# A written-out start, fillers on TensorE, and a chunk scan in steps of 4, 4, 4 and 2: one block of adaLN, state space and experts

## The chip, the core and the metric

The kernel runs on one core of a Trainium2 chip. The metric is device time in microseconds (us); lower is better. All data is float32.

## What is computed

Eight sequences of 512 tokens with 256 features each pass through two parts. Each part is wrapped in a modulation: six vectors per sequence are made of a conditioning row c, and the input is normalised, scaled, shifted, and the result is gated and added back.

```
mod = (silu(c) @ wmod).reshape(8, 6, 1, 256)          # sa ca ga sb cb gb
ga, gb = sign(ga) * max(|ga|, 0.25), the same for gb
h = layernorm(x) * (1 + ca) + sa
x = x + ga * mamba(h)
h = layernorm(x) * (1 + cb) + sb
x = x + gb * experts(h)

mamba(x):  xn = layernorm(x) * gamma + beta
           u, z = split(xn @ W_in.T)                    # 512 and 512
           xc = silu(causal_conv(u, 4 taps) + conv_b)
           state = state @ A.T + u_t @ Bm.T             # 16 numbers, 512 steps
           y_t = (xc_t + state @ Cm) * sigmoid(z_t)
           return x + y @ W_out.T
experts(x): softmax router over 8, the best one's two-layer gelu network, times a gate
```

## The kernel before

**Two halves.** The first half works on one sequence at a time ("batch" b, 0 to 7): `stage_norm` (L735, normalise, modulate, normalise, transpose to `xnT`), `stage_base` (L759, the residual and the gated output weights), `stage_conv` (L774, the state scan and the convolution), `stage_out` (L824, gate, output projection `po`, router) and `stage_place` (L899, where each token goes for its expert). The second half works through blocks of 256 or 128 tokens that belong to one expert: gather rows, two layers (`ph`, `py`), scatter the result. TensorE (PE) does the matmuls, VectorE (DVE) and ScalarE (ACT) the elementwise work and the emptying of PSUM, GpSimd (POOL) powers, residuals and the indirect DMAs, SyncE (SP) issues all other DMAs.

**The scan.** The 512 steps are cut into 128 chunks of CH = 4. `pv` gives each chunk's own contribution, 32 rows by 128 chunks, four of them stacked in `v`. What enters each chunk is then summed in steps with `SPAN` = (8, 4, 4) (L428, loop at L792): in the first step `pd` adds up the 8 chunks before each one with eight matmuls (weights `wb`), in the second three gaps of 8, 16, 24 chunks, in the third three gaps of 32, 64, 96 (weights `lm`). Each step ends with a DVE addition of `pd` into `v`, which the next step's matmuls read. `pc` then turns `v` into outputs. For weights the kernel needs powers of A: `states()` (L590) squares A repeatedly (`pa` into `at`), forms a few products more (`pmo`, `pm28`, into `more`), and lays them out (`lt`, `wb`, `lx`, `lm`, `cs`, `bw`). `pq`, `pw1`, `pm2`, `pw` and `pb` are the PSUM tiles of these.

**The modulation.** `three()` (L482) multiplies by one half of `wmod` (tiles `wm`): `pm` holds shift and scale, `pg` the gate. It is called for batch 0 alone on all partitions (`bc0`, from `s0`), and in `vectors()` (L513) for all eight rows, once per half; these go to memory as `mod_d` and `modb_d`. `stage_norm(b)` fetches its row of `mod_d` into `bc`. `vectors()` also computes sb, cb and ga with the features on the partitions (`pf`, six pieces of 128 features, two accumulating matmuls each, into `modT`), from which router weights `rw`, `rsum` and, by way of `wo` transposed, `pr` and `wr2`, come.

**Rows for the experts.** `xp_d` holds, per token, the row `xr` made by `stage_out` and a copy of the sequence's three modulation vectors, which a DMA from `modb_d` writes for a whole sequence at once (1536 KB). Before the change batch 0 issues those of sequences 0 and 1, batch b that of b + 1. The gathers of the first expert blocks, after batch 5, read what belongs to sequences 0 to 5.

**What sets the order.** Nothing is in the order of the code. The class `Plan` (L32) records every instruction of a half with a due time, what it depends on, and an estimated length (L92). `order()` (L191) then runs through them like a simulation: among the instructions whose inputs are there and whose buffer is free, the one that could start earliest is taken, and with equal starts the one due first. Each engine then executes its instructions in just that order. `nc.wanting(done=[...])` makes the planner wait for a tile as if the instruction read it. Batch b is due at (b + 3) * 36 us; `states()` and `vectors()` stand first, with a due time of 1e6 that what follows brings forward. PSUM tiles are taken by tag: `px` has three buffers, `tp` and `po` two each, `ps` one.

Of the kernel before, what the change touches and what calls it, by code (L numbers as in the profile page):

```python
# [35 lines left out]
class Plan:  # L36
# [20 lines left out]
    def __init__(self, tc, last=None):  # L57

        self.tc, self.nc = tc, tc.nc
        self.free = {q: last.free[q] if last else 0.0 for q in self.REACH}  # L60
        self.ops, self.touched, self.tiles = [], {}, {}
        self.due, self.also, self.pairing = 0.0, ([], []), 0
        for name in self.QUEUES:
            setattr(self, name, self.Engine(self, name))
# [71 lines left out]
    def add(self, name, op, args, kw):  # L136
# [19 lines left out]
        else:  # L156
# [6 lines left out]
            self.ops.append(me)  # L163
        if op == "activation":
            me["table"] = {AF.Gelu: 1, AF.Silu: 2, AF.Tanh: 2}.get(args[2] if len(args) > 2 else None)
        if "dma" in op:
            me["size"] = 4
            for _, n in out.ap:
                me["size"] *= n
            me["indirect"] = "indirect" in op  # L170
# [20 lines left out]
    def order(self):  # L191
# [19 lines left out]
        order, table = [], 2  # L211
# [14 lines left out]
        while len(order) < len(ops):  # L226
            best = None
            for q, l in ready.items():
                for o in l:
# [6 lines left out]
                    if best is None or (at, o["due"]) < best[:2]:  # L236
                        best = (at, o["due"], o)
            assert best is not None, "no buffer for any instruction that could be next"
            at, _, o = best
            table = o.get("table") or table  # L240

# [6 lines left out]
            free[o["queue"]] = at + o["length"]  # L248
            end = at + o["length"]
# [40 lines left out]
def adaln_mamba_moe_kernel(  # L290
# [137 lines left out]
    SPAN = (8, 4, 4)  # L428
    assert SPAN[0] * SPAN[1] * SPAN[2] == NC

    with tc.tile_pool(name="wa", bufs=1) as wa, tc.tile_pool(
# [81 lines left out]
        def vectors():  # L513

            for half, to in ((0, mod_d), (1, modb_d)):
                mod = wa.tile([B, 3, D], FP, name=f"mod{half}", tag="mod")
                three(mod, sT, half, B)
                nc.sync.dma_start(out=to, in_=mod.rearrange("b i d -> b (i d)"))


            pf = ps_o.tile([P, 6, B], FP, name="pf", tag="po")
            for m in range(6):
                w, at_m = (wmh[1], m) if m < 4 else (wmh[0], m)
                for k in range(KD):
                    nc.tensor.matmul(
                        pf[:, m], lhsT=w[:, k, at_m * P : (at_m + 1) * P],
                        rhs=sT[:, k, :], start=(k == 0), stop=(k == KD - 1),
                    )
            nc.vector.tensor_copy(modT[:, 0:2], pf[:, 0:2])
            nc.vector.tensor_scalar(modT[:, 2:4], pf[:, 2:4], 1.0, None, ALU.add)  # L530
            gT = modT[:, 4:6]
            nc.vector.tensor_copy(gT, pf[:, 4:6])
            mT = wa.tile([P, KD, B], FP, name="mT")
            nc.vector.scalar_tensor_tensor(mT, gT, -1.0, gT, ALU.mult, ALU.max)
            nc.vector.tensor_scalar(mT, mT, 0.25, None, ALU.max)
            nc.vector.tensor_scalar(gT, gT, 0.0, 2.0, ALU.is_ge, ALU.mult)
            nc.vector.scalar_tensor_tensor(gT, gT, -1.0, mT, ALU.add, ALU.mult)
# [52 lines left out]
        def states():  # L590


            for j in range(STEPS - 1):
# [5 lines left out]
                nc.vector.tensor_copy(at[:, j + 1], pa)  # L599
# [4 lines left out]
            nc.vector.tensor_copy(a3t, pa3)  # L604
# [6 lines left out]
            for i in range(CH):  # L611
                for j in range(i + 1):
                    nc.vector.tensor_copy(lt[:, i, j * SP : j * SP + DS], power[i - j])
                nc.vector.tensor_copy(lt[:, i, DS : 2 * DS], power[i + 1])
# [6 lines left out]
            more = wa.tile([DS, 6, DS], FP, name="more")  # L621
            pmo = ps_s.tile([DS, 5, DS], FP, name="pmo", tag="ps")
            for i, (l, r) in enumerate((
                (at[:, 3, 0], at[:, 2, 1]), (at[:, 4, 0], at[:, 2, 1]), (at[:, 4, 0], at[:, 3, 1]),
                (at[:, 6, 1], at[:, 5, 0]), (at[:, 8, 1], at[:, 7, 0]),
            )):
                nc.tensor.matmul(pmo[:, i], lhsT=l, rhs=r, start=True, stop=True)
            nc.vector.tensor_copy(more[:, 0:5], pmo)
            pm28 = ps_s.tile([DS, DS], FP, name="pm28", tag="ps")
# [759 lines left out]
```

## Time and profile before

| | us |
|---|---|
| median of 3 runs | 589.22 |
| lowest, highest | 585.32, 590.69 |
| the profiled execution | 587.33 |
| its span, first to last instruction | 585.2 |
| PE busy in the span | 562.3 |
| last `po` matmuls of batch 0 begin | 79.06 |
| last `po` matmuls of batch 7 begin | 313.46 |

The profile is of one execution. Its page has the span in 40 equal slices of 14.6 us, a digit giving tenths; "PEclk" is the TensorE clock that was granted. Timelines give start and duration in us, the engine, the line of the code that issued the instruction, the tiles and their shapes. All instructions that a plan records carry the line of the helper that records them (L154 or L159), so they are told apart by their tiles.

### The profile page before, as it was taken

What the parts mean: (1) busy time and instruction counts of PE and PEld (TensorE: products, weight loads), DVE (VectorE), ACT (ScalarE), POOL (GpSimd) and SP (SyncE); (2) the same over time, 40 slices, a digit from 0 to 9 for tenths busy, and PEclk for the clock granted to TensorE, in tenths of its full rate; (3) what the DMA queues carried; (4) which work ended last, traced back from release to release, by engine and by line L of the source; (5) the groups of instructions that cost most, each with busy time, mean ns of one, the idle gap of its engine ahead of it and who ended that gap; (6) DMA issues with size and microseconds to landing.
All of it is one profiled execution on the core that took longest, in us unless ns stands there. A gap on an engine that the chain in (4) does not pass through costs nothing.

```text
span 585.2 us, 8673 instructions
## 1 busy us (share of the span) xinstructions
PE 562.3 (96%) x2882; PEld 428.0 (73%) x2882; DVE 348.1 (59%) x1087; ACT 211.0 (36%) x404; POOL 209.3 (36%) x330
## 2 busy tenths in 40 slices
PE   4999999999999999999999798999999999999996
PEld 2454766757576676757578687878988988988895
DVE  4879968798987968686595924163433433522312
ACT  2328454455363445252342021222422222332140
POOL 1423673635446372621333421342242222322112
PEclk9779999999999999999999999999999999999999
DMA  7348999420210101010553969997887787886000
GB/s 277 129 129 183 271 254 258 71 91 0 64 38 1 38 2 36 1 37 1 161 175 91 239 198 398 394 396 266 282 279 275 274 251 242 276 286 194 15 18 20
DMA packets 58703, 96.73 MB, mean 165 GB/s; under 512 B 9852, under 2 KB 41854, under 8 KB 58656
## 3 DMA queue, kind: packets, MB, share of 16 engines
q1 hardware_dynamic: 50720, 72.98, 41.4%
q0 software_dynamic: 7936, 23.17, 11.1%
q8 instruction: 24, 0.39, 0.3%
q14 instruction: 23, 0.19, 0.2%
HBM read 86.42 MB, written 22.81 MB: 187 GB/s over the span
## 4 chain that ended last, share of the span: by engine, by line
PE 73%; DMA 17%; DVE 3%; issue 3%; SPq 1%; POOL 1%; ACT 0%; POOLq 0%; ACTq 0%
PE py L154 10%; PE px L159 10%; PE po L154 9%; PE px L154 9%; DMA out<-ot,ids 8%; PE ph L159 6%; PE ph L154 6%; PE pc L154 3%; PE po L159 3%; PE pd L154 3%; DMA ids<-ids_d 3%; DMA ids_d<-tok,row 2%; DMA w1t<-in_w 2%; PE py L159 2%; DMA xg<-xp_d,ids 1%
## 5 line engine op out<-in xcount | busy, mean ns | idle before, releaser
L159 ACT ACTIVATE gl<-ph,b1t 128x256 f32<-128x256 f32 (+1 forms) x152 | 68.3, 452 | 179.5 <-PE ph L154 159.9
L154 PE MATMUL py<-w2t,gl 128*128 128x256 f32 x476 | 108.3, 379 | 0.0
L154 PEld LDWEIGHTS py<-w2t,gl 128*128 128x128 f32 x476 | 90.4, 190 | 12.3
L159 PE MATMUL ph<-hT,w1t 128*128 128x256 f32 (+1 forms) x304 | 84.1, 358 | 5.4 <-DMA w1t<-in_w 3.0
L154 PE MATMUL ph<-hT,w1t 128*128 128x256 f32 (+1 forms) x304 | 83.8, 357 | 0.0
L159 POOL DMA_INDIRECT out<-ot,ids x36 | 36.4, 1012 | 130.7 <-DVE ot L159 121.0
L159 DVE TENSOR_TENSOR ot<-py,b2t 128x256 f32<-128x256 f32 x34 | 14.4, 424 | 113.0 <-PE py L154 113.0
L159 DVE SCALAR_TENSOR_TENSOR sv<-u,pt,sv 128x512 f32<-128x512 f32 x96 | 71.9, 759 | 4.3 <-ACT sv L159 4.3
L159 POOL DMA_INDIRECT xg<-xp_d,ids x36 | 38.9, 1080 | 87.3 <-DMA ids<-ids_d 48.3
L159 PE MATMUL px<-xnT,wi 128*128 128x512 f32 x128 | 69.6, 625 | 0.0
L154 PE MATMUL px<-xnT,wi 128*128 128x512 f32 x128 | 66.2, 599 | 0.0
L159 PEld LDWEIGHTS ph<-hT,w1t 128*128 128x128 f32 x304 | 54.4, 190 | 12.2 <-issue 3.6
L154 PEld LDWEIGHTS ph<-hT,w1t 128*128 128x128 f32 x304 | 55.3, 190 | 6.2
L154 PEld LDWEIGHTS px<-xnT,wi 128*128 128x128 f32 x128 | 24.6, 192 | 31.2 <-issue 31.2
L159 POOL DMA_INDIRECT ids_d<-tok,row x32 | 34.5, 1077 | 24.2 <-DVE row L159 13.2
L159 ACT COPY u<-px 128x512 f32<-128x512 f32 x32 | 18.7, 585 | 67.0 <-PE px L154 66.4
L159 ACT ACTIVATE tz<-px 128x512 f32<-128x512 f32 x32 | 19.0, 595 | 51.1 <-PE px L154 50.3
L159 POOL TENSOR_TENSOR rs<-ve,nhalf 128x4 f32<-128x4 f32 x16 | 18.8, 1174 | 44.9 <-DVE ve L159 32.2
L159 PEld LDWEIGHTS px<-xnT,wi 128*128 128x128 f32 x128 | 21.3, 192 | 17.4 <-issue 16.5
L159 DVE COPY hT<-tp 128x512 f32<-128x512 f32 (+1 forms) x20 | 12.7, 634 | 35.4 <-PE tp L154 27.4
L159 DVE TENSOR_TENSOR xr<-po,h 128x256 f32<-128x256 f32 x32 | 13.5, 423 | 30.6 <-PE po L154 30.4
L159 DVE TENSOR_TENSOR hg<-hg,xg 128x256 f32<-128x256 f32 x72 | 29.3, 421 | 1.1
(347 smaller groups left out, 949.8 us busy)
## 6 DMA issues: line engine op xcount, KB each, us to landing
w1t<-in_w SPq DMA_DIRECT2D x19, 1024.0 KB
w2t<-in_w SPq DMA_DIRECT2D x19, 1024.0 KB
xp_d<-modb_d SPq DMA_DIRECT2D x8, 1536.0 KB
xp_d<-xr SPq DMA_DIRECT2D x8, 520.0 KB
xt<-in_x SPq DMA_DIRECT2D x8, 512.0 KB
bc<-mod_d SPq DMA_DIRECT2D x7, 384.0 KB
b2t<-in_b SPq DMA_DIRECT2D x19, 128.0 KB
w<-in_w SPq DMA_DIRECT2D x2, 1024.0 KB
```

What stands on the lines that cost most here:

```text
L154: me["calls"].append(lambda: getattr(getattr(self.nc, name), op)(*args, **kw))
L159: calls=[lambda: getattr(getattr(self.nc, name), op)(*args, **kw)],
```

## The change

**The scan.** `SPAN` becomes (4, 4, 4, 2): four matmuls in the first step, then gaps of 4, 8, 12, of 16, 32, 48, and of 64. Other powers of A are prepared for it (seven weights in `lm` instead of six, four in `wb` instead of eight).

**The planner.** Three settings are new. Up to `hold` (24 us of the plan's time) an engine prefers, among instructions that could start within 0.3 us of its first, the one due first. Up to `thick` (100 us) PE, where the columns streamed in the last 3.4 us plus those of the next instruction are below 1800, takes a dense instruction if one could start within 0.3 us. `warm` inserts matmuls without use (`pwarm`, 128x256, the identity) into PE's planned gaps before 20 us, for 80% of each gap, and reckons PE at half speed before 7.8 us.

**The start.** `stage_norm(0)` is recorded first, due at 20 us. `vectors()` and `stage_base(0)` wait, in the plan, for batch 0's `xnT`. `pf` is no longer computed from `wm`, but transposed from the rows that `three()` made. The small copies in `states()` move from DVE to ACT, and three PSUM tiles there from tag `ps` to `px`.

**The modulation copies.** Those for sequences 0 to 7 are issued by batches 1, 2, 3, 3, 4, 4, 5 and 5, and wait in the plan for that batch's `xr`.

```diff
@@ Plan.add
+        if queue == "PE":
+            n = 1
+            for c in ins[1 if op == "matmul" else 0].shape[1:]:
+                n *= c
+            me["dense"] = me.get("dense", 0) + (2 if op == "matmul" else 1) * n * ins[0].shape[0] / P
...
+            if ins and ins[0].space == DRAM and out.space == DRAM:
+                me["size"] *= 2
@@ Plan.order
-                    if best is None or (at, o["due"]) < best[:2]:
-                        best = (at, o["due"], o)
+                    could.append((at, o["due"], o["i"], o))
+                if could:
+                    mine = min(could)
+                    if mine[0] < self.hold:
+                        mine = min((c for c in could if c[0] < mine[0] + 0.3), key=lambda c: c[1:3])
+                    if q == "PE" and mine[0] < self.thick:
+                        t, l = mine[0], mine[3]["length"]
+                        lately = sum(
+                            d * max(0.0, b - max(a, t + l - 3.4)) / (b - a) for a, b, d in streamed[-40:]
+                        )
+                        if lately + mine[3]["dense"] < 1800:
+                            dense = [c for c in could if c[3]["dense"] > 900 * c[3]["length"] and c[0] < t + 0.3]
+                            mine = min(dense, key=lambda c: c[1:3]) if dense else mine
+                    if best is None or mine[:3] < best[:3]:
+                        best = mine
...
+            length = o["length"]
+            if self.warm and o["queue"] == "PE" and at < self.warm[0]:
+                slow = 2 if at < self.warm[1] else 1
+                n = int(0.8 * (at - free["PE"]) / (slow * self.warm[2]))
+                if n > 0:
+                    order.append(dict(i=-1, at=free["PE"], queue="PE", calls=[self.warm[3]] * n))
+                    streamed.append((free["PE"], at, 512 * n))
+                    fillers += 1
+                length *= slow
@@ scan
-    SPAN = (8, 4, 4)
+    SPAN = (4, 4, 4, 2)
@@ vectors()
+            pf = ps_o.tile([P, 6, B], FP, name="pf", tag="po")
             for half, to in ((0, mod_d), (1, modb_d)):
+                nc.due = (1 + 2 * half) * PERIOD
                 mod = wa.tile([B, 3, D], FP, name=f"mod{half}", tag="mod")
                 three(mod, sT, half, B)
                 nc.sync.dma_start(out=to, in_=mod.rearrange("b i d -> b (i d)"))
-            pf = ps_o.tile([P, 6, B], FP, name="pf", tag="po")
-            for m in range(6):
-                w, at_m = (wmh[1], m) if m < 4 else (wmh[0], m)
-                for k in range(KD):
-                    nc.tensor.matmul(
-                        pf[:, m], lhsT=w[:, k, at_m * P : (at_m + 1) * P],
-                        rhs=sT[:, k, :], start=(k == 0), stop=(k == KD - 1),
-                    )
...
+                for m, i in ((0, 1), (2, 0)) if half else ((4, 2),):
+                    for k in range(KD):
+                        nc.tensor.transpose(
+                            pf[:, m + k], mod[:, i, k * P : (k + 1) * P], ident[0:B, 0:B]
+                        )
+            nc.due = 3 * PERIOD
+            nc.vector.tensor_copy(modT, pf)
@@ states(): the copies of at, a3t, lt, more, wb, lx, ix, lm and bw
-                nc.vector.tensor_copy(at[:, j + 1], pa)
+                nc.scalar.copy(at[:, j + 1], pa)
...
-            more = wa.tile([DS, 6, DS], FP, name="more")
-            pmo = ps_s.tile([DS, 5, DS], FP, name="pmo", tag="ps")
+            more = wa.tile([DS, 3, DS], FP, name="more")
+            pmo = ps_s.tile([DS, 3, DS], FP, name="pmo", tag="ps")
...
-            pm28 = ps_s.tile([DS, DS], FP, name="pm28", tag="ps")
-            nc.tensor.matmul(pm28, lhsT=at[:, 4, 0], rhs=more[:, 0], start=True, stop=True)
-            back = [i16, at[:, 2, 1], at[:, 3, 1], more[:, 0], at[:, 4, 1], more[:, 1], more[:, 2],
-                    more[:, 5]]
+            back = [i16, at[:, 2, 1], at[:, 3, 1], more[:, 0]]
...
-            gaps = [at[:, 5, 0], at[:, 6, 0], more[:, 3], at[:, 7, 0], at[:, 8, 0], more[:, 4]]
+            gaps = [at[:, 4, 0], at[:, 5, 0], more[:, 1], at[:, 6, 0], at[:, 7, 0], more[:, 2], at[:, 8, 0]]
@@ stage_place
-            for n in range(b + 1 if b else 0, min(b + 2, B)):
-                nc.sync.dma_start(
-                    out=xp_d[n * L : (n + 1) * L, OWN:ROW], in_=modb_d[n].partition_broadcast(L)
-                )
+            for n in ((), (0,), (1,), (2, 3), (4, 5), (6, 7), (), ())[b]:
+                with nc.wanting(done=[xr]):
+                    nc.sync.dma_start(
+                        out=xp_d[n * L : (n + 1) * L, OWN:ROW], in_=modb_d[n].partition_broadcast(L)
+                    )
@@ the loop over batches
+        pwarm = ps_o.tile([P, 2, P], FP, name="pwarm", tag="po")
+        twice = ident.unsqueeze(1).to_broadcast([P, 2, P])
+        plan.hold, plan.thick = 24.0, 100.0
+        plan.warm = (20.0, 7.8, 0.47, lambda: chip.tensor.matmul(
+            pwarm, lhsT=ident, rhs=twice, start=True, stop=True
+        ))
+        nc.due = 20.0
+        t = stage_norm(0)
+        nc.due = 1e6
         cs, wb, lm, bw = states()
-        rw, rsum, wr2 = vectors()
+        with nc.wanting(done=[t["xnT"]]):
+            rw, rsum, wr2 = vectors()
+            nc.due = 3 * PERIOD
+            stage_base(t)
         for b in range(B):
             nc.due = (b + 3) * PERIOD
-            t = stage_norm(b)
-            stage_base(t)
+            if b:
+                t = stage_norm(b)
+                stage_base(t)
             stage_conv(t)
```

## The prediction

> **What bounds the kernel now.** I read the busy shares first, then the busy time by stretch, then TensorE's (PE's) instructions in order of time where the clock or the idle time stood out. The page:
>
> ```profile
> PE 562.3 (96%) x2882; PEld 428.0 (73%) x2882; DVE 348.1 (59%) x1087; ACT 211.0 (36%) x404; POOL 209.3 (36%) x330
> PE   4999999999999999999999798999999999999996
> PEclk9779999999999999999999999999999999999999
> PE 73%; DMA 17%; DVE 3%; issue 3%; SPq 1%; POOL 1%; ACT 0%; POOLq 0%; ACTq 0%
> ```
>
> PE is busy for 562.3 of 585.2 us, so about 23 us are idle: some 8 before 8 us, under 1 from there to 40 us, 3 in 40 to 320 us, 6 at the handover to the experts (320 to 400 us), 6 at the end. A change helps if it takes work from PE, raises its clock, or closes one of these holes. The clock row shows a loss in the second and third slice. The start by stretch (columns as headed):
>
> ```profile
> core 0: us, PE busy (x) PEld busy (x) DVE busy (x) ACT busy (x) POOL busy (x), PEclk, DMA share, GB/s
> 0.00:8.00 8.00, 0.59 (x9) 0.41 (x10) 5.45 (x34) 1.50 (x2) 1.35 (x15) 1.00 0.67 223
> 8.00:14.00 6.00, 6.00 (x17) 1.96 (x18) 0.46 (x3) 2.07 (x4) 1.38 (x10) 1.00 0.91 350
> 14.00:20.00 6.00, 6.00 (x47) 4.88 (x48) 5.73 (x21) 1.07 (x2) 0.10 (x1) 1.00 0.90 338
> 20.00:27.20 7.20, 7.20 (x19) 1.51 (x18) 5.57 (x24) 3.25 (x6) 4.25 (x5) 0.53 0.01 2
> 34.00:40.50 6.50, 6.50 (x21) 4.58 (x20) 4.65 (x21) 0.59 (x1) 1.02 (x1) 0.51 0.83 226
> ```
>
> Two stretches run at a granted clock of 0.53 and 0.51: lost 7.2 x 0.47 + 6.5 x 0.49 = 6.6 us. What ran ahead of each, and what the first wide matmuls took (timeline: start, duration, instruction, count; an fp32 matmul shows as two records):
>
> ```profile
> 9.98 2.08 PE L159 MATMUL pm<-wm,s 128*128 128x512 f32 x2
> 11.85 1.90 PE L154 MATMUL pm<-wm,s 128*128 128x512 f32 x2
> ...
> 16.19 2.60 PE L154 MATMUL pf<-sT,wm 128*128 128x8 f32 x22
> ...
> 34.49 3.15 PE L154 MATMUL pb<-pt,wxo 128*128 128x16 f32 x14
> 37.48 2.05 PE L159 MATMUL px<-xnT,wi 128*128 128x512 f32 x2
> 39.33 1.82 PE L154 MATMUL px<-xnT,wi 128*128 128x512 f32 x2
> 41.07 0.39 PE L159 MATMUL pw<-ident,lt 16*128 16x16 f32 x2
> ```
>
> At 10 us a pm of four records took 3.8 us although the clock row says 1.00, as much as px at 37.5 us under 0.51; at 285 us px takes 1.72. So 8 to 14 us ran at half rate as well (about 3 us lost). Both drops of the clock come behind a PE that the profile calls fully busy, but with matmuls only 8 or 16 columns wide. The first px of batch 0 starts at 37.5 us although its input xnT was there at 32.1 us.
>
> The scan over chunks in a later batch, ending each time where px starts:
>
> ```profile
> 289.08 0.41 PE L159 MATMUL pd<-v,wb 128*32 128x127 f32 x2
> 289.32 1.63 PE L154 MATMUL pd<-v,wb 128*32 128x126 f32 x14
> 290.88 1.12 PE L159 MATMUL px<-xnT,wi 128*128 128x512 f32 x2
> ...
> 293.16 0.39 PE L159 MATMUL pd<-v,lm 32*32 32x120 f32 x2
> 293.39 0.53 PE L154 MATMUL pd<-v,lm 32*32 32x112 f32 x4
> 293.85 1.13 PE L159 MATMUL px<-xnT,wi 128*128 128x512 f32 x2
> ...
> 295.76 0.35 PE L159 MATMUL pd<-v,lm 32*32 32x96 f32 x2
> 295.95 0.33 PE L154 MATMUL pd<-v,lm 32*32 32x64 f32 x4
> 296.21 1.12 PE L159 MATMUL px<-xnT,wi 128*128 128x512 f32 x2
> ```
>
> Eight matmuls 1.80 us, then three in 0.69, then three in 0.45, nothing idle around them.
>
> **The change, part by part**, against the profiled execution's own 587.33 us (span 585.2 and 2.1 around it; the median of the runs is 589.22, 0.3% above). Since PE bounds all but the holes, I sum PE's time.
>
> (1) Spans 4, 4, 4, 2. The first step loses four of eight matmuls: half of 1.80, -0.90 per batch. The later ones go from six matmuls with 528 columns to seven with 712: 184 columns more, at 0.112 us per 128-column record and two records, 0.32 at most, 0.16 if the half of it hides under the weight loads; and one more group between px's, whose switch costs about the 0.2 by which px ahead of 290.88 and behind it takes 1.9 instead of 1.72. Net -0.5 per batch, -4.0 in eight (bounds -2.5 and -5.5). The fourth step adds one VectorE add per batch (0.23 us by the 32x96 row) and one more round trip. It is covered by the px's between the steps, as the three now are; without the cover a trip is some 0.6 us, 5 us in all.
>
> (2) Less work ahead of the loop. pf: 24 records in 2.7 us become six narrow transposes, about 0.12 each by the tp_a rows, -2.0. pw1 halves: -0.95 of 1.9. pmo and pm28 lose about 0.25, pm2 gains 0.1. Sum -3.1 (bounds -2 and -4).
>
> (3) The clock. With pf gone, and wide instructions preferred where few columns went through lately, the first drop should go. pb's 16-column matmuls, 1.7 us at full clock, and the tiny 16x16 ones stay and will stand closer together, so a later or shorter drop is likely. I take -4 of the 6.6 lost (bounds 0 and -6.6).
> The Trainium skill, "TensorE: Matmul & The Clock Gate", section "What's actually happening", has the clock fall after an idle window of about 3.4 us and tells the modeller that the ramp is under 1% of a span and not to fit a cold count. That speaks against this part: PE is nowhere idle that long after 8 us, so by the page the choice of wide instructions earns nothing and my sum would be 580.7; but the trace has the clock at 0.53 right behind 6.00 busy of 6.00, so I go by the rows.
>
> (4) The filling matmuls. They sit only where the plan sees PE idle before 20 us, in 80% of each gap, at 0.47 us (0.94 cold). They can warm PE ahead of 8 us and so save the 3 us lost at half rate. But between the powers of A the plan's gaps (a copy of some 0.2 us with its two hand-overs) are shorter than one cold filler over 0.8, 1.2 us, so few may fit. I take -1.5 (bounds 0 and -3).
>
> (5) The new order. Batch 0's normalisation goes first: xt lands at 5.6 and wm at about 8 us, then pm 1.9 us, VectorE 0.8 + 1.2 + 1.2 + 1.75, the POOL power 1.1, ScalarE 2.1, transposes and xnT 1.5: near 20 to 23 us instead of 32. Until then only states() can feed PE: pm and pg 2.9, wi transposes 0.9, pq 4.2, powers 1.7, pb 1.7, pw1 1.0, pm2 0.7, 13 us for the 14 available, partly waiting on copies. All of vectors() now stands behind xnT (pg, pm 5.8, pf 0.7, wo transposes 0.9, psc 0.8, pr 2.0), interleaved with px. This removes no work; I charge 2 us of new idle time (bounds 0 and 8). Queued behind: the row of batch 1's modulation, mod_d, goes through SyncE to memory and back into bc, at 33.3 and 35 us now, about as late as then; its reader is at 55 us.
>
> (6) 34 small copies go from VectorE to ScalarE. On VectorE they take about 0.11 each back to back, 3.7 us. ScalarE's small row is 0.22 (ct), so 7 us beside its 11 busy of 40 us: it costs nothing while ScalarE has that room; if not, each late copy holds PE by up to 0.2 us, inside the bounds of (5). VectorE is the next limit: 55 us busy by 72 us now. Taking off 4, and the start of its work at 5.6 us, batch 0 cannot end much before 60 us instead of 72; that allows the 11 us I count.
>
> (7) The eight 1536 KB copies of modulation rows leave 42 to 93 us, where they take 6.3 us each, for batches 1 to 5, two at a time in three of them. SyncE then holds xt and bc for up to 13 us; bc is issued at 152 and read at 183 us. Nothing, with that 31 us as the cover.
>
> Handover and end move along with the first part; I leave them, +-1.5 us. Sum: -4.0 - 3.1 - 4 - 1.5 + 2 = -10.6, so 587.3 - 10.6 = 576.7 us.
>
> **Rivals.** A, the work goes but the clock does not recover: narrow work bunched before 20 us takes the clock down just as the px's begin. Against it: pf is gone. (3) and (4) at 0, (5) at +4: 587.3 - 7.1 + 4 = 584.2, within 1%.
> B, all of it is gained: -4 - 3.1 - 6.6 - 3 and no new idle time, 570.6. For it: PE's idle time from 8 to 40 us is already under 1 us, so work can move up. Against: VectorE's limit in (6).
> C, slower, by the fillers alone: PE works in order, so a filler planned for a gap that the chip does not have delays the next real matmul. Between 8 and 20 us the plan can see up to 12 us of gaps, 9.6 us of fillers at its 0.47; if the clock stays at half rate there, as it did up to 14 us, they take 0.94 each, 19 us in all, and if the real work is late none of it falls into a hole: 587.3 - 7.1 + 19 = 599. It decides from where the delay exceeds the 7.1 of (1) and (2), and shows as slower from 15 us. For it: the plan's times are estimates. Against: xt and wm land at 5.6 and 8 us, early in the span, and states() has 13 us of real work for just these gaps.
>
> **How the numbers follow.** Forecast (571 to 583) 0.61; B 0.13; A (583 to 595) 0.17; C 0.09. One per cent of 589.22, about what a measurement can tell, is 5.9 us: faster means below 583.3, slower above 595.1. The forecast's and B's chances make 0.74 faster; A makes 0.17 same; C 0.09 slower. The range from 567 to 589 leaves out the lower half of B's tail (0.07) and C with the upper part of A (0.13). The likeliest case's own range is 571 to 583.
>
> **What would show it.** (1) pd steps of about 0.9, 0.7, 0.55 and 0.3 us, with px between. (2) No pf from wm. (3) PEclk 9 or more from the second slice on; a 7 there says A. (4) pm near 10 us taking 1.9 instead of 3.8 us. (5) The first px near 22 us, no idle PE over 1 us before 80 us. C would show pwarm records directly ahead of late pm records. The prediction fails if the first px still starts near 35 us, or if batch 0's last po does not move from 79 us to below 70.

## The result, and the profile after

The changed kernel takes 605.24 us (median of 4 runs, 600.67 to 607.01) against 588.36 us before (585.32 to 590.69): the ratio is 1.028 [1.020, 1.036], slower. The forecast was 576.7 us. The profiled execution took 600.67 us, its span is 598.9 us (before 585.2).

The same four lines of the page as shown of before (busy time; PE and its granted clock in 40 slices; the chain):

```profile
PE 567.5 (95%) x2816; PEld 427.8 (71%) x2816; DVE 360.7 (60%) x1054; ACT 215.0 (36%) x439; POOL 207.8 (35%) x330
PE   8799999889999999999979998989999999999996
PEclk9789999889999999999979998999999999999999
PE 54%; DMA 21%; DVE 13%; issue 6%; ACT 2%; POOL 1%; SPq 1%; another core or an unknown queue 1%; POOLq 0%; DVEq 0%; ACTq 0%
```

PE's busy time contains 5.24 us of fillers; without them it is 562.3 us, just what it was. Inside it things moved: `pd`, `pm`, `pg`, `pf`, `pb`, `pq` and `pw` cover 11.9 us less than before, and `pc`, `px`, `tp_a` and `po` 9.4 us more, the largest part `pc` (28.6 to 33.0 us); how much of that is a lower clock (below) was not separated. The loss is idle time: 598.9 - 562.3 = 36.6 us hold no useful matmul, against 22.9 before, and that is the whole 13.7 us of the span. The chain says the same: PE's share fell from 73 to 54%, VectorE's rose from 3 to 13%, DMA's from 17 to 21%. The waits of PE (total, times, longest) name the new holes:

```profile
PE pc L160 <- DVE v L160: 4.1, 3, 3.5
PE pd L160 <- DVE v L160: 3.3, 2, 2.8
PE pf L160 <- DVE mod L160: 2.9, 2, 2.6
PE po L160 <- DVE lg L160: 2.6, 1, 2.6
```

Of before, no wait of PE for `v` is in the list. Where the time lies is read from the end of each batch's last `po` matmul (us from the start of the span; the row below has how much shorter (-) or longer (+) each batch got):

| batch | 0 | 1 | 2 | 3 | 4 | 5 | 6 | 7 | the rest |
|---|---|---|---|---|---|---|---|---|---|
| end, before | 79.6 | 113.9 | 149.3 | 181.8 | 213.7 | 247.0 | 281.0 | 314.0 | 585.2 |
| end, after | 74.7 | 118.1 | 155.3 | 190.0 | 220.8 | 256.8 | 287.1 | 326.8 | 598.9 |
| batch's gain or loss | -4.9 | +9.1 | +1.8 | +2.2 | -1.1 | +2.7 | -3.7 | +6.7 | +0.9 |

The start gains, batches 1 and 7 lose 15.8. The border between two batches is not sharp: batch 1 now holds 37 `px` records and batch 2 28, before 32 and 37, so part of batch 1's loss is work that moved ahead of the border. Batches 0 to 2 together lose 6.0 us.

**The start** (timeline of PE; start, duration, instruction, count, and idle time with its releaser):

```profile
1.71 5.24 PE L1128 MATMUL pwarm<-ident 128*128 128x256 f32 x12 [1.71 <-POOL seen L160]
7.72 1.10 PE L160 MATMUL pm<-wm,s 128*128 128x512 f32 x2 [0.77 <-DMA wm<-in_wmod]
8.65 1.02 PE L155 MATMUL pm<-wm,s 128*128 128x512 f32 x2
...
24.93 1.13 PE L160 MATMUL px<-xnT,wi 128*128 128x512 f32 x2
```

The fillers run ahead of 7 us, `pm` takes 1.95 us instead of 3.8, and the first `px` starts at 24.9 instead of 37.5 us.

**The scan** in batch 7, to be held against the steps of before:

```profile
295.13 0.40 PE L160 MATMUL pd<-v,wb 128*32 128x127 f32 x2
295.37 0.80 PE L155 MATMUL pd<-v,wb 128*32 128x126 f32 x6
...
298.38 0.39 PE L160 MATMUL pd<-v,lm 32*32 32x124 f32 x2
298.62 0.56 PE L155 MATMUL pd<-v,lm 32*32 32x120 f32 x4
...
301.02 0.37 PE L160 MATMUL pd<-v,lm 32*32 32x112 f32 x2
301.24 0.46 PE L155 MATMUL pd<-v,lm 32*32 32x96 f32 x4
...
303.98 0.29 PE L160 MATMUL pd<-v,lm 32*32 32x64 f32 x2
```

Four steps of 0.97, 0.73, 0.61 and about 0.3 us up to the next `px`, for 1.80, 0.69 and 0.45. All `pd` records of the span cover 20.6 us of PE, before 23.6 (what the record ahead of each still covers is not counted).

**Batch 7** (timeline, several engines): the copies of the modulation rows of sequences 6 and 7, the read of the token lists, the first experts' rows, and who waits for them; last, the clock by stretch:

```profile
267.54 1.60 SPq L160 DMA_DIRECT2D xp_d<-modb_d  x2
...
271.41 1.08 POOL L160 DMA_INDIRECT ids_d<-tok,row  x1 [2.54 <-DVE v L160]
...
298.39 4.16 SPq L1055 DMA_DIRECT2D ids<-ids_d  x4
...
307.25 0.41 DVE L160 TENSOR_SCALAR hg<-xg 128x256 f32<-128x256 f32 x1 [4.63 <-DMA xg<-xp_d,ids]
...
308.04 0.20 DVE L160 TENSOR_TENSOR v<-v,pd 32x64 f32<-32x64 f32 x1
...
308.39 0.77 PE L160 MATMUL pc<-v,cs 128*128 128x128 f32 x2 [3.53 <-DVE v L160]
...
306.00:314.00 8.00, 5.46 (x24) 5.20 (x24) 3.08 (x8) 0.00 (x0) 5.60 (x24) 0.57 1.04 356
```

And the same read of the lists before:

```profile
279.22 4.16 SPq L1029 DMA_DIRECT2D ids<-ids_d  x4
```

The copies go out at 267.5 us, right ahead of batch 5's scatters of token numbers (`ids_d`). SyncE can read the lists back only at 298.4 us, 11.3 us behind the end of batch 6; before, that was at 279.2, 1.8 us ahead of it. The planner has put `hg`, which needs the gathered rows, into VectorE's queue ahead of the scan's `v`. So VectorE waits 4.63 us for rows, `v` stands behind, and PE waits 3.53 us for `v`. From 306 to 314 us the granted clock is 0.57 besides. The DMA view of 262 to 302 us (last column: median us from issue to landing, of the landings that the trace knows; here two of the four scatters, 16.9 and 23.9 us):

```profile
xp_d<-modb_d SPq DMA_DIRECT2D x2, 1536.0 KB, 15.7
...
ids_d<-tok,row POOLq DMA_INDIRECT x4, 20.4
```

**VectorE beside POOL** (timeline around 125 us, in batch 2):

```profile
124.55 4.14 DVE L160 SCALAR_TENSOR_TENSOR sv<-u,pt,sv 128x512 f32<-128x512 f32 x3
...
125.13 2.35 POOL L160 TENSOR_TENSOR h<-h,xt 128x1024 f32<-128x1024 f32 x1
...
128.69 0.27 DVE L160 TENSOR_TENSOR v<-v,pd 32x127 f32<-32x127 f32 x1
...
129.01 0.39 PE L160 MATMUL pd<-v,lm 32*32 32x124 f32 x2 [2.79 <-DVE v L160]
```

Three `sv` that take 0.75 us each elsewhere take 4.14 together, while POOL multiplies 1024 elements beside them; `v` stands behind them, and PE waits 2.79 us. A plainer case of the same kernel, in batch 1:

```profile
83.14 2.38 POOL L160 TENSOR_TENSOR h<-h,xt 128x1024 f32<-128x1024 f32 x1
...
83.26 2.31 DVE L160 TENSOR_TENSOR eq<-eq,prio 128x32 f32<-128x32 f32 x1
```

`eq`, a 128x32 product of 0.19 us, lasts until POOL is done. I call VectorE's time beyond the median of the same form "stretched": 27.0 us in 18 instructions after, 15.6 us in 14 before, each beside a wide POOL product. In batch 1 it is 6.4 us, before 0.8.

**Batch 1.** From 74.7 to 118.1 us PE is idle for 4.6 us, before 0.6 (79.6 to 113.9). None of this is a wait for `v`. The holes are 1.07 us ahead of `pk` at 88.3, 0.95 ahead of a `pc` at 95.9 and 2.62 ahead of a `po` at 111.8 us. In the chain ahead of the first stands the `eq` just shown. The largest does not come from POOL, which has nothing to do from 105.8 to 113.6 us; it hangs on an `xr` that starts late, for a reason that is open (under "Left open"). The other 5.1 us of the loss are busy time of PE: the `px` records that moved there, and a granted clock of 0.96 (1.00 before).

**The clock** follows the holes (stretches; column PEclk):

```profile
105.00:112.00 7.00, 4.38 (x25) 3.83 (x24) 2.23 (x8) 1.14 (x2) 0.84 (x4) 1.00 0.00 0
112.00:115.00 3.00, 3.00 (x10) 2.32 (x9) 2.64 (x11) 1.24 (x3) 0.16 (x3) 0.56 0.00 0
115.00:129.00 14.00, 11.22 (x41) 6.31 (x39) 13.19 (x22) 5.53 (x10) 8.62 (x6) 0.97 0.12 31
129.00:132.00 3.00, 2.99 (x9) 1.61 (x10) 3.00 (x15) 1.05 (x3) 1.27 (x3) 0.58 0.46 163
```

Behind each of these two holes (2.62 us ahead of 111.8, 2.79 ahead of 129.0) PE runs some 3 us at 0.56 to 0.58. Over the span the mean granted clock is 0.976 (before 0.987).

### The profile page after: what moved, and what is told of

It reads as the page before. It is cut to its first block, busy times and chain, and to the rows that moved or that the text cites. A ratio compares the mean times of both kernels' runs of the same rounds, so it can differ in the third digit from the quotient of the medians.

```text
span 598.9 us, 8561 instructions
## 1 busy us (share of the span) xinstructions
PE 567.5 (95%) x2816; PEld 427.8 (71%) x2816; DVE 360.7 (60%) x1054; ACT 215.0 (36%) x439; POOL 207.8 (35%) x330
## 4 chain that ended last, share of the span: by engine, by line
PE 54%; DMA 21%; DVE 13%; issue 6%; ACT 2%; POOL 1%; SPq 1%; another core or an unknown queue 1%; POOLq 0%; DVEq 0%; ACTq 0%
DMA xg<-xp_d,ids 11%; PE py L155 10%; PE po L155 7%; PE px L160 6%; PE px L155 6%; PE ph L160 6%; PE ph L155 6%; DVE sv L160 5%; DMA ids_d<-tok,row 4%; DMA ids<-ids_d 3%; PE pc L155 2%; PE po L160 2%; DMA w1t<-in_w 2%; DVE st L160 2%; DVE ve L160 2%
## 5 line engine op out<-in xcount | busy, mean ns | idle before, releaser
L160 DVE TENSOR_TENSOR ot<-py,b2t 128x256 f32<-128x256 f32 x34 | 14.4, 425 | 114.3 <-PE py L155 114.3
L160 DVE SCALAR_TENSOR_TENSOR sv<-u,pt,sv 128x512 f32<-128x512 f32 x96 | 75.5, 802 | 7.7 <-ACT sv L160 6.8
L160 PE MATMUL px<-xnT,wi 128*128 128x512 f32 x128 | 70.8, 635 | 0.2 <-DVE sv L160 0.2
L160 POOL DMA_INDIRECT xg<-xp_d,ids x36 | 40.2, 1117 | 83.4 <-DMA ids<-ids_d 26.1
L155 PE MATMUL px<-xnT,wi 128*128 128x512 f32 x128 | 66.8, 604 | 0.0
L155 PEld LDWEIGHTS px<-xnT,wi 128*128 128x128 f32 x128 | 24.9, 194 | 31.5 <-issue 31.5
L160 ACT ACTIVATE tz<-px 128x512 f32<-128x512 f32 x32 | 19.0, 594 | 49.2 <-PE px L155 32.3
L160 POOL TENSOR_TENSOR rs<-ve,nhalf 128x4 f32<-128x4 f32 x16 | 17.6, 1101 | 40.0 <-DVE ve L160 36.7
```

What stands on the lines that cost most here:

```text
L155: me["calls"].append(lambda: getattr(getattr(self.nc, name), op)(*args, **kw))
L160: calls=[lambda: getattr(getattr(self.nc, name), op)(*args, **kw)],
```

## The experiments

Each row is one kernel: its median, its ratio to the kernel before on the same chip (the comparison's own, with its interval, and not the quotient of two medians; the medians of before lie between 586.1 and 587.6 us), and of its profile the length of batches 0, 1 and 7 and the end of batch 7's last `po`, all in us.

| kernel | median | ratio [95%] | batch 0 | batch 1 | batch 7 | end |
|---|---|---|---|---|---|---|
| e1_span_only | 620.94 | 1.057 [1.052, 1.063] | 81.0 | 64.6 | 30.5 | 350.1 |
| e2_old_span | 603.96 | 1.029 [1.024, 1.035] | 85.4 | 34.2 | 43.5 | 330.5 |
| e3_old_copies | 601.87 | 1.025 [1.020, 1.030] | 73.7 | 39.0 | 32.6 | 328.7 |
| e4_no_fill | 606.03 | 1.033 [1.028, 1.038] | 77.4 | 40.2 | 42.6 | 333.2 |
| e5_scan_copies | 603.23 | 1.028 [1.018, 1.038] | 79.9 | 35.6 | 39.7 | 327.3 |
| e6_split_pool | 595.50 | 1.013 [1.005, 1.021] | 71.9 | 38.7 | 44.9 | 326.9 |
| e7_before_split | 584.65 | 0.998 [0.995, 1.001] | 74.3 | 34.3 | 32.9 | 308.4 |
| e8_copies_earlier | 592.51 | 1.010 [1.003, 1.018] | 71.3 | 42.9 | 33.9 | 317.3 |
| e9_split_early | 586.00 | 0.996 [0.993, 0.999] | 70.5 | 38.5 | 32.7 | 312.9 |
| e10_copies_only | 593.30 | 1.010 [1.006, 1.014] | 78.9 | 37.9 | 33.7 | 317.0 |
| e11_scan_early | 593.78 | 1.011 [1.007, 1.016] | 80.0 | 34.5 | 32.7 | 320.9 |
| e12_old_span_early | 592.03 | 1.004 [1.000, 1.009] | 85.2 | 34.2 | 32.4 | 319.2 |
| e13_lock_after | 593.53 | 1.013 [1.009, 1.017] | 70.8 | 34.8 | 31.6 | 314.7 |
| e14_lock_before | 615.99 | 1.050 [1.044, 1.056] | 82.8 | 53.6 | 33.1 | 339.1 |
| e15_lock_old_span | 586.60 | 1.001 [0.998, 1.005] | 70.7 | 34.8 | 33.4 | 312.8 |
| e16_old_span_split | 580.51 | 0.988 [0.985, 0.991] | 78.1 | 34.2 | 32.3 | 313.0 |
| e17_lock_split | 582.73 | 0.992 [0.989, 0.995] | 69.4 | 34.9 | 33.1 | 310.2 |

**One part at a time (e1 to e5, e10, e11).** The theories at the outset: S, the fourth step of the scan costs a round trip; O, the new order at the start and its settings; C, the copies in pairs hold up batch 7.

e1 is the kernel before with the scan alone:

```diff
-    SPAN = (8, 4, 4)
+    SPAN = (4, 4, 4, 2)
```

> The kernel before with only the scan in steps of 4, 4, 4 and 2 (and the powers of A it needs, copied on VectorE as before). If the fourth step is what costs (theory S: one more round trip of TensorE and VectorE in every batch, which the px's do not cover), this is slower than before by 8 us or more, with waits of pd or pc for v. If the scan only takes work from TensorE (theory O: the loss comes from the new order and start), this is 3 to 6 us faster than before, near 584 us.

e2 is the changed kernel with the scan put back, the same two lines the other way round.

> The changed kernel with the scan back in steps of 8, 4 and 4, the rest of the change kept. Theory S: near 590 us or below, most of the 17 us recovered. Theory O: 600 us or more, since the start, the planner's settings and the moved copies stay, and about 4 us of matmuls come back.

e3 is the changed kernel with the old rule for the copies:

```diff
-            for n in ((), (0,), (1,), (2, 3), (4, 5), (6, 7), (), ())[b]:
-                with nc.wanting(done=[xr]):
+            for n in range(b + 1 if b else 0, min(b + 2, B)):
```

> The changed kernel with the copies of modulation rows issued as before (sequences 0 and 1 by batch 0, then b + 1, without waiting for xr). Theory C (two copies at a time hold back the ids and the gathers behind batch 5, so that VectorE waits some 8 us for xg in batch 7): batch 7's period falls from 39.7 to about 33 us and the whole to about 594 us. If the copies are hidden (my prediction's point 7): no difference, 600 us or more.

e4 is the changed kernel without fillers and without the choice of dense instructions:

```diff
-        plan.hold, plan.thick = 24.0, 100.0
-        plan.warm = (20.0, 7.8, 0.47, lambda: chip.tensor.matmul(
...
+        plan.hold = 24.0
```

> The changed kernel without the filling matmuls and without the preference for dense instructions; hold, the new order of the start, the scan and the moved copies stay. Theory O in the form that the preference disturbs the batches up to 100 us: batches 1 and 2 take about 34 us each again instead of 43 and 37, the whole near 590 us, with 2 or 3 us lost at a slower start. If the preference is harmless: batch 0 ends 3 us or more later than at 74.7 us, and the whole is 603 us or more.

e1 came out far slower than either theory had it, by a mishap of its order. From the waits of e1 (all engines):

```profile
DVE st L159 <- DMA xt<-in_x: 29.2, 2, 27.7
...
PE po L154 <- DVE sv L159: 26.0, 2, 25.5
```

The input `xt` stands behind the 1536 KB copies, VectorE waits 27.7 us for it and PE 25.5 us for VectorE. It says little of the scan, but a lot of the method: a new scan means a new order of everything. e2, e3 and e4 each stay at +2.5 to +3.3%, so no single part carries the loss. e3 shows batch 7 at 32.6 us with the old copies, and batch 2 at 50.6 instead: for C, but not clean. e4's `pm` waits 7.6 us for its weights and takes 3.96 us (2.05 + 1.91), after 1.95: the fillers do what the prediction said. Batch 0 ends 2.7 us later (77.4 for 74.7), which is within what one plan gives from execution to execution (74.7 here, 71.3 in e8), and in the total the intervals overlap.

So the next kernels keep a plan as it is, or change the fewest parts. e5 is the kernel before with the scan and the new rule of the copies (old start, old planner):

> The kernel before with the new scan (4, 4, 4, 2) and the new rule for the copies of the modulation rows (in pairs, after the residual); the start, the modulation and the planner's settings are those of before. Theory S (the fourth step of the scan costs the middle batches by itself, through one more round trip between TensorE and VectorE a batch): the six periods of batches 1 to 6 sum to 208 us or more (201.4 before, 212.4 after), the time is 597 to 606 us. Theory O (the middle batches lose only by the order that the new start and settings bring): the six periods sum to 199 to 204 us, the time is 580 to 592 us. Both expect no wait of 20 us for a DMA as in e1_span_only, since the copies are spread out again.

Batches 1 to 6 take 207.7 us in all (201.4 before), and 603 us is what S expected; but 6.7 us of it are batch 7, 39.7 as in the changed kernel. The loss needs neither the new start nor the fillers. The next two single out the suspects, with every engine's order but one left alone.

**POOL's products in pieces (e6, e7).** Four instructions of 256 elements in place of one of 1024:

```diff
+            if queue == "POOL" and op == "tensor_tensor" and len(out.shape) == 3 and out.shape[2] == 256:
+                me["calls"] = [
+                    lambda n=n: self.nc.gpsimd.tensor_tensor(out[:, n], args[1][:, n], args[2][:, n], args[3])
+                    for n in range(out.shape[1])
+                ]
```

> The changed kernel, same order on every engine, but each wide product of POOL (128 partitions x 4 x 256) is issued as four instructions of 256 elements. Theory P (VectorE is stretched for as long as one wide POOL product runs beside it, because it is held to the end of the POOL instruction): the stretched VectorE time falls from 27 us to 10 us or less, batch 1 gets shorter by 3 us or more, the time is 592 to 600 us. Rival (the two engines share a rate, and the length of the instruction does not matter, or the stretch lies beside other work): the stretch stays at 20 to 30 us and the time at 602 to 609 us.

> The kernel before with the same split of POOL's wide products. Theory P: 15.6 us of stretched VectorE time in before falls to 6 us or less; since TensorE bounds its batches, the time falls by only 0 to 4 us, 582 to 588 us. Rival (a shared rate, or more instructions on POOL cost more): 586 to 592 us.

**The copies of 6 and 7 earlier (e8)**, moved in SyncE's queue alone:

```diff
+        copies = [o for o in order if o.get("copy")]
+        if copies:
+            for o in copies[6:]:
+                order.remove(o)
+            at = order.index(copies[3]) + 1
+            order[at:at] = copies[6:]
```

> The changed kernel with the same order on every engine but SP's queue, in which the copies of sequences 6 and 7 are issued right behind those of 2 and 3 (by some 200 us instead of 267 us). Theory C (these two copies hold back the scatters of batch 5, so the gathers of batch 7's first experts, and TensorE waits in batch 7): the period of batch 7 falls from 39.7 us to 33 to 34.5 us, the half-clock episode at 306 us goes, the time is 597 to 600 us. Rival (batch 7 is long for the order of its own work, or the copies hold up something else where they are now): period 7 stays above 38 us, or another batch grows by as much, and the time is 603 to 608 us.

e8 is the clearest: batch 7 falls from 39.7 to 33.9 us, and the ratio from 1.028 to 1.010. SyncE's part of the timeline of e8:

```profile
198.26 5.95 SPq L160 DMA_DIRECT2D xp_d<-modb_d  x4
...
228.25 4.72 SPq L160 DMA_DIRECT2D xp_d<-modb_d  x2
...
285.50 4.18 SPq L1062 DMA_DIRECT2D ids<-ids_d  x4
```

And the scatters in e8's DMA view of the same 40 us as above (last column: median us to landing):

```profile
ids_d<-tok,row POOLq DMA_INDIRECT x8, 9.3
```

The lists are read 2.1 us behind the end of batch 6 (11.3 after). The 9.3 us are the middle of two known landings of different batches, 6.1 us for the first scatter of batch 5 and 12.5 for the first of batch 6; like for like, the first scatter of batch 5 lands in 6.1 us for 16.9 after. The gain in the median, more than was expected, is in part batch 0's (71.3 for 74.7 in the same plan, a difference between executions).

e6 shortens batch 1 by 4.7 us and the time to 595.5, as theory P had it, but its mechanism is shown only in part: the stretched time falls to 20.5, not 10 us. What goes from batch 1 is mostly the hole ahead of `po` (2.62 us, none in e6), which was not POOL's; batch 2 grows by 2.6 us, and batch 7 to 44.9. So the profiled execution, the slowest of e6's four, ends batch 7 where the changed kernel did (326.9 and 326.8), and the gain stands in the medians alone. Why the stretch remains is in its successor e9 below. e7 gains nothing that can be told from no change, and its stretched time falls from 15.6 to about 10 us, not to the 6 of theory P.

**The repairs together (e9), and the other cross-checks (e10, e11, e12).** e9 is e6's edit and e8's edit on the changed kernel; e10 is the kernel before with the new rule of the copies alone; e11 is e5 with e8's edit; e12 is e2 with e8's edit.

> The changed kernel, same plan, with both single edits of before: POOL's wide products in pieces of 256 elements, and the copies of sequences 6 and 7 issued behind those of 2 and 3. The two losses lie in different batches (1 and 7), so if both are what they seemed, the gains add: batch 1 at 38.5 to 39.5 us, batch 7 at 33 to 34.5 us, 580 to 589 us, about level with the kernel before (586.8). Rival (the split only moves the loss from batch 1 into batch 2, which grew from 37.2 to 39.7 us with it): 589 to 594 us, no better than the earlier copies alone (592.5).

> The kernel before with the new rule for the copies of the modulation rows alone: old scan, old start, old planner. Theory C (two copies at a time behind batch 5's residual hold back its scatters, the read of the lists and the first gathers): batch 7 takes 37 us or more (33.0 before), the time is 590 to 598 us. Rival (batch 7 was long only in the order that came with the scan or the start): batch 7 stays at 32.5 to 34 us, 582 to 589 us; it may even gain, since the copies leave the first 90 us.

> The kernel before with the new scan and the new copies as in e5_scan_copies, same plan as there, but the copies of sequences 6 and 7 issued behind those of 2 and 3. With batch 7 repaired, what is left against before is the scan itself on the old start. Theory S (the fourth step costs the middle batches): batch 7 33 to 34.5 us, batches 1 to 6 still 206 to 209 us in all (201.4 before), 592 to 599 us. Rival (the scan costs nothing, the sum of the middle batches in e5_scan_copies came from the copies too): batches 1 to 6 at 202 us or less, 582 to 588 us.

> The changed kernel with the old scan (8, 4, 4), plan of e2_old_span, and the copies of sequences 6 and 7 issued behind those of 2 and 3. Theory C: batch 7 falls from 43.5 us to 33 to 35 us. Theory S on top: batches 1 to 6 stay at 200 to 203 us (new scan 212), so this version stands at 580 to 590 us, below the changed kernel with the earlier copies (592.5). Rival (the scan is not to blame, batch 1 is long for its place behind the new start): batches 1 to 6 stay near 201.6 as measured, but what is saved there is lost in batch 0, which took 85.4 us in that plan, and the time is 590 to 597 us.

In e9 the gains add: the ratio goes from 1.028 to 0.996. e11 and e12 repeat theory C on two more plans: batch 7 from 39.7 to 32.7 and from 43.5 to 32.4 us. With batch 7 out of the way e11 still takes 208.2 us for batches 1 to 6 and 593.8 in all, as S expected; e12 takes 201.6 for them, but 85.2 for batch 0, as its rival had it. e10 did not put the case of C: in its plan the copies of 4 to 7 all go out from 230.6 us on, and batch 7 takes 33.7. It is 1.0% slower all the same, 3.0 us of it in batches 1 to 6 (204.4), for reasons I did not follow. But it takes from e11 its proof of S: with the old scan, the same start and the new rule of the copies e10 takes 593.3 us, e11 with the new scan and e8's edit 593.8 (ratios 1.010 and 1.011). The timeline of e9 in batch 2:

```profile
136.18 2.77 POOL L167 TENSOR_TENSOR h<-h,bc 128x256 f32<-128x256 f32 x4
136.24 5.48 DVE L160 SCALAR_TENSOR_TENSOR nm<-mv,rs 128x4 f32<-128x4 f32 x1 [0.91 <-POOL rs L160]
...
138.90 0.09 POOL L160 MEMSET sl_at<- 1x1 f32 x1
138.95 2.75 POOL L167 TENSOR_TENSOR h<-h,xt 128x256 f32<-128x256 f32 x4
```

`nm`, 0.15 us elsewhere, is kept out for eight POOL products in a row, 5.48 us, and ends with the last of them. That is not the rule either: in e16 (below), at 249.05 us, four VectorE instructions in a row took 0.68 to 0.77 us each beside four such pieces of `wb` that followed each other, so each was held for one piece only. What decides between the two is not shown.

**A planner that knows of the exclusion (e13 to e15)**: e8, the kernel before, and e12, in that order, with

```diff
+            me["pair"] = queue == "DVE" or (queue == "POOL" and length > 2.0)
...
+                    if o.get("pair"):
+                        at = max(at, paired["POOL" if q == "DVE" else "DVE"])
...
+            if o.get("pair"):
+                paired[o["queue"]] = at + o["length"]
```

where a `pair` is an elementwise instruction with all operands in SBUF.

> The changed kernel with the earlier copies of sequences 6 and 7, and a planner that does not start a VectorE instruction with all operands in SBUF beside a wide POOL product, nor the other way round (new order throughout). Theory P (batches 1 and 2 are long because VectorE is held off beside POOL): stretched VectorE time falls from 23.7 us to under 12 us, batches 0 to 2 end at 143 to 148 us instead of 151.4, the time is 580 to 588 us (592.5 without). Rival (VectorE's load and the fourth round trip make them long): the stretch falls, but batches 0 to 2 end at 150 us or later, and the time is 590 to 597 us.

> The kernel before with the same knowledge in its planner. Theory P: stretched VectorE time falls from 15.6 us to under 8 us; TensorE bounds its batches, so the time falls by 0 to 5 us, 582 to 587 us. Rival (each new order costs something by itself, since the plan's times are only estimates): 588 to 597 us.

> As e13_lock_after, but with the old scan (8, 4, 4). Theory S (the scan's fourth step costs): 2 us or more below e13_lock_after. Prediction's own sum (the new scan saves 4 us of TensorE): 2 to 6 us above e13_lock_after. Neither: within 2 us of it, the 3 us of matmuls saved are lost again in waiting.

A miss: the stretched time does not fall (23.2, 28.5 and 23.7 us). I take it that the plan's times are too rough to keep two engines apart by a microsecond; that is not shown. So these runs say nothing for or against theory P. e14 is 5% slower than before for its new order alone; in its list of waits PE stands still for 9.5 us in one piece, `pk` for `xr`.

e15 against e13, old scan against new, is 586.6 to 593.5, as S expected, but not where S looks for it. Of the 8.4 us between their profiled spans 6.5 lie behind batch 7 (the rest takes 270.9 and 277.4 us; PE of e13 waits there 2.27 and 5.33 us for `hg`), and batch 7 ends at 312.8 and 314.7 us.

**A version below both (e16, e17)**: e6's edit on e12 and on e15. Both have the old scan.

> The changed kernel with the old scan, the earlier copies and POOL's products split (plan of e12_old_span_early). In that plan TensorE never waits for the scan's addition on VectorE. Theory S (the fourth step's waits cost about what its matmuls save): within 3 us of e9_split_early, 583 to 589 us. Prediction's own sum (the new scan saves 4 us): 588 to 592 us. If the split helps here as it did in the changed plan (6 us), 583 to 587 us.

> e15_lock_old_span with POOL's products split as well. If VectorE is still held off in that plan (23.7 us stretched) and the split frees it in part, 579 to 584 us, which would be below both kernels; if the stretched VectorE time there lies beside TensorE's work, 585 to 588 us, no change.

e16 takes 580.5 us, 1.2% [0.9, 1.5] below the kernel before and below every range expected of it. Its stretched time is 8.3 us (25.2 in e12, its plan unsplit), and here the trace shows where PE gains by it: over e12 the profiles gain in batch 0 (85.2 to 78.1 us), where e12 has, among other holes,

```profile
75.82 0.71 PE L155 MATMUL po<-wb__203,sv 128*128 128x264 f32 x2 [2.04 <-DVE sv L160]
```

behind an `sv` that is stretched to 2.23 us, and e16 has no such wait. e16 is e9 with the old scan, and the first waits of PE in e16 (total, times, longest) have none for `v`, nor has the rest of the list:

```profile
PE ph L160 <- DMA w1t<-in_w: 3.2, 2, 1.8
PE pwarm L1145 <- POOL seen L160: 1.7, 1, 1.7
PE pd L160 <- ACT wb L160: 1.3, 1, 1.3
PE pf L160 <- DVE mod L160: 1.1, 1, 1.1
```

## Why the prediction was wrong

**(7), the copies, "Nothing, with that 31 us as the cover": failed.** I checked only `bc`'s place in SyncE's queue. The copies' own traffic was not priced: two of 1536 KB ahead of batch 5's scatters keep the first of these in flight for 16.9 instead of 6.1 us, and the read of the lists, the gathers, `hg`, `v` and `pc` hang on them. e8 alone takes the ratio from 1.028 to 1.010, 10 us, of which batch 7 has 5.8 in the profiles; batch 7 came down in all four kernels where the copies were moved, by 5.8, 12.2, 7.0 and 11.1 us (e8, e9 against e6, e11 against e5, e12 against e2). The term was put at 0.

**VectorE beside POOL: missing from the sum.** (6) weighed VectorE by its busy time. 34 copies did leave it and it still got busier, 348.1 to 360.7 us; 11.4 of these 12.6 us are instructions that stood still beside POOL, 27.0 us for 15.6. Splitting POOL's products brought 1.5, 1.4, 1.6 and 0.9 per cent (the differences of the ratios of e6 and the changed kernel, e9 and e8, e16 and e12, e17 and e15; of the first pair the intervals touch, of the others they are apart), and nothing on the kernel before (e7): there, behind 10 us, PE never waits longer than 0.63 us for VectorE. So the cost is shown by the splits. Where it fell is shown for the hole at 129.0 us of the changed kernel and the one of e12 above, and not for the largest hole of batch 1. The Trainium skill, "SBUF — State Buffer", section "Who interferes with whom", says that a VectorE instruction with two inputs in SBUF contends with a POOL instruction that reads SBUF, since the two engines share a pair of ports that is locked exclusively. Of VectorE's 2-port modes it adds that whoever issues first has the pair for the whole instruction and the other blocks fully. The trace agrees (`eq` 2.31 for 0.19 us), and the `xr<-po,h` that read PSUM kept their 0.42 us inside such products. Six of the 18 stretched instructions are `ve<-mv`, which has one input in SBUF. In one place the trace goes further than that: `nm` was kept out across eight instructions in a row (5.48 us).

**(1), the scan: the matmuls right, the cover wrong.** `pd` fell by 3.0 us (23.6 to 20.6) where I had 4.0 less in all. But "it is covered by the px's between the steps, as the three now are" failed: PE waits 7.4 us for `v` after (part of it by the copies and by POOL, above), 3.9 in e8, 3.2 in e9, and not at all in before, e2, e7, e10, e12 and e16. The addition is short (0.20 to 0.27 us), but it stands in VectorE's queue behind `sv`, `hg` or a blocked instruction. Such waits are not the new scan's alone: e14, e15 and e17 have the old one and 3.5, 3.7 and 3.0 us of them. Old scan against new, all else kept but the order that follows from it, by the ratios: e2 1.029 and 1.028, e12 1.004 and 1.010 (e8; the intervals overlap), e15 1.001 and 1.013 (e13), e16 0.988 and 0.996 (e9). By the profiles batch 7 ends at 319.2 and 317.3 us (e12, e8), 312.8 and 314.7 (e15, e13), 313.0 and 312.9 (e16, e9). So the gain of 0.7% that the sum had came in no pair. That the new scan costs something by itself is not shown: twice the whole is clearly slower, but with an order of its own each time, and for e13 mostly behind the scans.

**(2) held**: `pf` 2.6 to 0.9, `pw` 4.1 to 3.4, `pmo` 0.34 to 0.27 us, -2.5 of the -3.1. **(4) held** in mechanism (`pm`, above). **(3), the clock, -4: failed.** A drop remains, now at 16 to 22 us (0.57), and new drops came with the new holes. By the mean granted clock the share that was not granted rose from 7.6 to 14.4 us of the span (estimates: 0.013 of 585.2, 0.024 of 598.9). In e8, where the hole of batch 7 is gone, the mean is 0.987 again, as before. That the clock follows holes of 2.6 us here is shorter than the 3.4 us of the page the prediction cites; the row decides.

**(5), the order, +2 us: too small.** Batch 0 ends at 74.7, not below 70, and `pf` waits 2.63 us at 29.7 us for `mod`, which VectorE ends late. The range's ends were worked out for the start alone; of rival C only its sign was right, its mechanism was not: the fillers fall into holes.

Summed for the profiled execution: -4.9 in batch 0, +9.1 in batch 1 (4.0 of it idle PE, the larger part of that unexplained; the rest work moved from batch 2, and the clock), +1.9 in batches 2 to 6 (with the 2.79 us for `v` beside POOL), +6.7 in batch 7 (the copies, with the clock behind them), +0.9 behind. The two repairs together (e9) bring the kernel back to before, 0.996 [0.993, 0.999]. The expected gain was 1.8%; why the rest of it does not come is open, and e9's waits for `v`, 3.2 us, are a part of it at most.

**Left open.** In batch 1 of the changed kernel `xr` starts 4 us behind the last matmul of its `po`, without a releaser that the trace knows:

```profile
106.46 0.51 PE L155 MATMUL po<-rw,baseT 128*128 128x8 f32 x4
...
111.17 0.42 DVE L160 TENSOR_TENSOR xr<-po,h 128x256 f32<-128x256 f32 x1 [4.16 <-remote]
111.81 0.68 PE L160 MATMUL po<-wb__279,sv 128*128 128x264 f32 x2 [2.62 <-DVE lg L160]
...
113.64 0.10 POOL L160 MEMSET u<- 128x3 f32 x1 [7.79 <-DVE sv L160]
```

Its wait is 4.16 us here, 3.60 in e8 and 1.53 in e6. No DMA moves data then, and POOL is idle. The semaphore that it waits for last is raised by PE's instructions alone; as far as the trace's records go it is raised at 105.30 us and next at 111.15, though they show `po`'s matmuls as done by 109.2. Why is open. I made no experiment on it. What new order costs by itself (e1, e10, e14) isn't settled either, and it lies under every comparison of the two scans.

## What to carry to other kernels

Price a moved transfer by what runs beside it and what hangs on that, not only by its place in its own queue: 3 MB ahead of a 1 KB list cost 6 to 12 us in batch 7, by the plan. Where VectorE and POOL both work on SBUF operands, look for VectorE instructions that outlast their form's median before adding short ones that PE waits for; a shorter chain of matmuls with one more hand-over to an in-order queue need not gain, and brought nothing here. And where a planner orders everything, test one part with the order frozen, or the order's own few per cent hide it.

## What was not expected of the hardware

- A VectorE instruction of 0.15 us took 5.48 us beside eight POOL products that followed each other (e9); one POOL product of 1024 elements held others for 2.3 us.
- With two copies of 1536 KB in flight a small scatter issued behind them on another queue took 16.9 us to land, and 6.1 with the copies moved away (the first of batch 5, after and e8).
- Two holes of 2.6 and 2.8 us of PE were each followed by about 3 us at a granted clock of 0.56 to 0.58.
